# Moving one quarter of a tile's maxima and two query copies ahead of a value copy, and one cast from ScalarE to GpSimd

## The chip, the cores and the metric

The kernel runs on one core of a Trainium2 chip. The core has five engines that run side by side and meet at semaphores: TensorE (PE in the profile; PEld is its weight load), VectorE (DVE), ScalarE (ACT), GpSimd (POOL) and SyncE (SP, which here only issues DMAs). TensorE writes its results to PSUM, which has eight banks of 128 x 512 float32; the other data lies in SBUF. The metric is the time of one execution on the device, in microseconds, as the median of several runs; lower is better.

## The reference

A cross-attention layer with a residual and a layer norm, all in float32: four batches of 2048 query rows and 77 context rows, width 512, 16 heads of 32.

```python
qs = (x @ wq).reshape(B, 2048, 16, 32).transpose(0, 2, 1, 3)
ks = (ctx @ wk).reshape(B, 77, 16, 32).transpose(0, 2, 1, 3)
vs = (ctx @ wv).reshape(B, 77, 16, 32).transpose(0, 2, 1, 3)
scores = einsum('bhqd,bhkd->bhqk', qs, ks) / sqrt(32)
scores = where(mask, -inf, scores)
attn = einsum('bhqk,bhkd->bhqd', softmax(scores), vs)
out = attn.transpose(0, 2, 1, 3).reshape(B, 2048, 512) @ wo + x
return (out - mean(out)) / sqrt(var(out) + 1e-5) * gamma + beta
```

## The kernel before

The 8192 query rows are 64 tiles of 128 rows. Two tiles make a block, four tiles a group: the query projection runs by groups, scores and softmax by tiles, the product with the values by blocks. Large products are made in three passes: each float32 operand is split into a rounded high part (float32r) and the rest, and high x high, high x low and low x high are added up in one PSUM bank. So each piece of the transposed input is first cast (the high part, on ScalarE) and then subtracted (the low part, on GpSimd).

The order of the work is written out by hand. `ORDER` is a long string of words, and the program issues them one after the other; each engine runs its own part of them strictly in that order, and waits at semaphores only where data or a buffer is not ready. A word is a letter and a number, for some with a part behind a dot. Those that matter here:

- `Qn`: TensorE projects one quarter (128 columns) of a query group into a PSUM bank, n = 4 x group + quarter. `qn`: VectorE copies that bank to SBUF (line 305). `q5` and `q7` are the quarters 1 and 3 of group 1, which is tiles 4 to 7.
- `Sn`: TensorE makes the scores of tile n (line 428). Its outer loop runs over the four query quarters, so the second round needs quarter 1. The scores of a tile fill four banks; the inner loop `j` runs over these banks.
- `Tn.p`: VectorE adds the mask to a quarter of tile n's heads and takes the negated row maxima, four heads, each one instruction and a short read of its accumulator (line 445). A part empties one of the tile's four banks. `en.p`: ScalarE's exponentials of that quarter (line 460).
- `rn`, `nn`, `tn`: reciprocal (VectorE, line 470), normalising multiplication (GpSimd, line 475) and 32x32 transposition (VectorE, line 496) of tile n. `Pb.i` is one of twelve small DMAs that regroup a block's transposed weights into the tile `PT` (line 507); the ending `s` says that SyncE issues it.
- `Bn`: TensorE projects the values into a bank (line 353; line 341 for the left-over rows of `B2`). `Dn`: VectorE copies that bank to SBUF (line 360). `Zn`: a DMA puts rows of that copy in their place in `vsb` (line 372).
- `Gn`: VectorE makes the low part of `wo` (line 396). `gn`: SyncE loads half a group of the transposed input. `in`: the cast of that half (`cast_xT`, line 270), n = 2 x group + half. `jn`: GpSimd's subtraction for it (line 274). `i7` is the second half of group 3.
- `On`, `Vb`, `+n` are the output projection, the product with the values and the residual of the main stretch.

PSUM banks and SBUF buffers are handed out in the order of the calls by a fixed table (`SLOTS`); TensorE must wait until the last reader of a bank is done before it writes the bank anew. By that table the scores of tile 4 (`S4`) take as their fourth bank that of `B0`, which `D0` empties. `S6` takes the banks of `Q7`, of a quarter of tile 3's scores (the one that `T3.0` reads), of `Q5` and of `B2`. `B1` takes the first bank of `S4`, which `T4.0` empties.

Of the kernel before, what the change touches and what calls it, by code (L numbers as in the profile page):

```python
# [9 lines left out]
F32R = mybir.dt.float32r  # L10
# [7 lines left out]
P = 128  # L18
# [11 lines left out]
NC_D = D // P  # L30
BLK = 256
GRP = 2 * BLK
# [19 lines left out]
E l0 l2 R1 R0 R3 C2 C0 C1 C3 g5 M4.4 A0 M0.1 M12.4 A1 M1.3 A3 M8.4 K2 A2 H2 J3 p K0 g4 J1 i3 i2 S0 I2 j2 S1 T0.1 e0.1  # L52
T0.2 H0 T0.0 j3 e0.0 T1.0 T0.3 e0.2 T1.1 Q4 T1.2 e0.3 F0 T1.3 I0 e1.2 r0 n0 S2 q4 e1.0 S3 T2.3 T2.0 Q7 i5 T2.1 e1.3 F2
T2.2 j5 t0 e1.1 Q6 i4 F1 g7 r1 Y1 e2.0 F3 L1 T3.2 n1 Q5 x1 T3.1 e2.1 Y0 q6 R2 T3.3 e3.3 j4 t1 B0 e2.3 P0.6s x3 e3.1 B2
D0 i7 q7 Z0.s T3.0 P0.10s e3.0 q5 P0.2s S4 P0.7s D2 e3.2 Z3.s S6 T4.0 P0.4s e2.2 G1 B1 g6 G2 Z1.s G0 Z2.s T4.3 e4.3
P0.3s r3 G3 P0.0s Q9 n3 T4.1 P0.1s T4.2 e4.2 P0.9s D1 P0.8s r2 n2 e4.0 t3 P0.5s Q8 P0.11s e4.1 T6.0 T6.3 i6 t2 Q10
e6.0 r4 P1.0s T6.2 n4 P1.8s T6.1 e6.1 S5 P1.2s q10 x2 q8 Q11 e6.2 j6 P1.11s T5.3 P1.1s T5.2 e5.3 P1.10s T5.1 P1.9s t4
j7 e6.3 P1.4s S7 P1.6s Q14 T7.0 P1.7s e7.0 q9 P1.3s r6 T7.3 P1.5s n6 e7.3 T7.2 x0 q11 Q13 g8 e7.2 T5.0 Z13.s T7.1 g9
# [120 lines left out]
def xattn_layernorm(  # L179
# [15 lines left out]
    nc = tc.nc  # L195
# [12 lines left out]
    def buf(shape, dtype, tag, name):  # L208
        pool = tiny if shape[-1] <= H else sb
        return pool.tile(shape, dtype, tag=tag + next(slots[tag]), name=name)  # L210

    def once(held, key, shape, dtype, tag):
        if key not in held:
            held[key] = buf(shape, dtype, tag, f"{tag}_{key}")
        return held[key]
# [42 lines left out]
    fx, xh, xl, qd, qp, pts, m8s, mbs = {}, {}, {}, {}, {}, {}, {}, {}  # L258
# [6 lines left out]
    def load_xT(g, c):  # L265
        fx[g, c] = buf([P, 2, GRP], F32, "xtf", name=f"xtf_{g}_{c}")
        nc.sync.dma_start(fx[g, c], xT[g, :, c : c + 2])

    def cast_xT(g, c):
        nc.scalar.copy(once(xh, g, [P, NC_D, GRP], F32R, "xth")[:, c : c + 2], fx[g, c])  # L270

    def split_xT(g, c):
        l = once(xl, g, [P, NC_D, GRP], F32R, "xtl")
        nc.gpsimd.tensor_tensor(l[:, c : c + 2], fx.pop((g, c)), xh[g][:, c : c + 2].bitcast(F32), ALU.subtract)  # L274
# [19 lines left out]
    def q_visit(g, m):  # L294
        pq = qp[g, m] = bank(f"pq_{g}_{m}")
        if g:
            q_rows(pq, m, g, slice(0, GRP))
        else:
            for i in range(2):
                q_rows(pq[:, i * BLK : (i + 1) * BLK], m + i, 0, slice(BLK, GRP))  # L300

    def q_evac(g, m):
        pq = qp.pop((g, m))
        if g:
            nc.vector.tensor_copy(once(qd, g, [P, NG, GRP], F32, "q")[:, m, :], pq)  # L305
        else:
            nc.vector.tensor_copy(qd[0][:, m : m + 2, BLK:], pq.rearrange("p (m r) -> p m r", m=2))
# [456 lines left out]
    for c in range(0, NC_D, 2):  # L764
# [11 lines left out]
        "L": lambda k, part: load_mask(k), "M": mask_bias,  # L776
        "l": lambda k, part: nc.sync.dma_start(fx[1, k], xT[1, :, k : k + 2]),
        "g": lambda k, part: load_xT(k // 2, k % 2 * 2),
        "i": lambda k, part: cast_xT(k // 2, k % 2 * 2), "j": lambda k, part: split_xT(k // 2, k % 2 * 2),
        "Q": lambda k, part: q_visit(*divmod(k, 4)), "q": lambda k, part: q_evac(*divmod(k, 4)),  # L780
        "S": lambda k, part: scores(k), "T": lambda k, part: maxima(k, q4 * part, q4 * part + q4),
        "e": lambda k, part: exps(k, q4 * part, q4 * part + q4), "r": lambda k, part: recip(k),
# [73 lines left out]
```

## Time and profile before

| what | value |
|---|---|
| median of 3 runs | 507.34 us (507.14 to 507.61) |
| the profiled execution | 507.4 us, its span 505.6 us |
| mean granted TensorE clock | 0.994 |
| PE busy | 495.3 us, 98% of the span |
| DVE busy | 468.3 us, 93% |
| ACT busy | 474.1 us, 94% |
| POOL busy | 414.2 us, 82% |
| chain that ended last | PE 82%, DVE 12%, POOL 3% |

The span goes from the first to the last instruction that the profile holds; the execution's own time is 1.8 us longer. Busy time of PE counts matmuls whose ends are modelled, so a short wait can be partly covered by the modelled end of the matmul ahead of it. In the timelines each row starts with the start (us from the start of the span) and the duration; a bracket at the end gives the idle time of the engine ahead of the row and what ended it. Rows of one engine overlap a little, since an instruction's write-back is still counted while the next one has begun; the pitch from start to start tells what one costs in a row of several. One matmul of line 428 leaves two records in the trace (64 in all for the scores of a tile).

### The profile page before, as it was taken

The numbers are of one execution on the slowest core, as the hardware profiler recorded it, in microseconds if no ns is written. First come the engines' busy times: TensorE is split into PE (matmuls) and PEld (weight loads), VectorE is DVE, ScalarE is ACT, GpSimd is POOL, SyncE is SP. The second block draws the span as 40 slices with busy tenths as digits, with TensorE's granted clock in tenths as the row PEclk, the third lists the DMA queues.
The fourth block names the chain that finished last, engine by engine and source line by source line (L and its number), as shares of the span: only waits on it lengthen the run. The fifth ranks groups of instructions, "written<-read, shape, count | busy, mean of one in ns | idle before, by whom it ended". The sixth has DMA issues, their size and how long they took to land.

```text
span 505.6 us, 21827 instructions
## 1 busy us (share of the span) xinstructions
PE 495.3 (98%) x6834; PEld 383.1 (76%) x6834; DVE 468.3 (93%) x2556; ACT 474.1 (94%) x2253; POOL 414.2 (82%) x379
## 2 busy tenths in 40 slices
PE   9999999999999999999999999999999999999993
PEld 6987777777777787777777777777877777877672
DVE  6797999999999999999999999999999999999995
ACT  6699999998999999999999999999999999999972
POOL 3663756999978998988899898889989769889894
PEclk9999999999999999999999999999999999999997
DMA  8947767878987777777777777778777788678656
GB/s 312 396 151 213 177 188 179 240 193 234 258 234 216 213 221 200 219 231 232 212 208 221 208 200 234 226 211 241 223 195 234 199 229 236 182 205 203 182 172 252
DMA packets 59521, 110.97 MB, mean 219 GB/s; under 512 B 9441, under 2 KB 12283, under 8 KB 59410
## 3 DMA queue, kind: packets, MB, share of 16 engines
q1 hardware_dynamic: 56658, 103.99, 70.8%
q0 software_dynamic: 2224, 5.05, 3.6%
q8 instruction: 60, 0.98, 0.9%
q10 hardware_dynamic: 528, 0.52, 0.4%
q14 instruction: 51, 0.42, 0.3%
HBM read 41.79 MB, written 16.78 MB: 116 GB/s over the span
## 4 chain that ended last, share of the span: by engine, by line
PE 82%; DVE 12%; POOL 3%; issue 1%; DMA 1%; ACT 1%; DVEq 0%; POOLq 0%
PE pq L291 31%; PE po L602 28%; PE sc L428 9%; PE pa L521 9%; DVE pbuf L445 4%; DVE B L496 3%; PE pk L314 1%; PE pq L745 1%; PE pv L353 1%; DVE q L305 1%; DVE AL L554 1%; POOL pbuf L475 1%; DMA first_xtl<-xw 1%; POOL PT L507 1%; POOL xth L641 1%
## 5 line engine op out<-in xcount | busy, mean ns | idle before, releaser
L460 ACT ACTIVATE pbuf<-pbuf,nm 128x77 f32<-128x77 f32 x1024 | 352.5, 351 | 3.4 <-DVE nm L445 3.3
L460 ACT ACTIVATION_READ_ACCUMULATOR pbuf<-pbuf,nm 128x1 f32 x1024 | 195.7, 191 | 0.0
L445 DVE CUSTOM_DVE_ANT_0 pbuf<-sc,mb 128x77 f32<-128x77 f32 x1024 | 171.1, 233 | 6.9 <-PE sc L428 3.7
L475 POOL TENSOR_TENSOR pbuf<-pbuf,ri 128x1232 f32<-128x1232 f32 x63 | 142.8, 2268 | 32.0 <-DVE ri L470 30.7
L602 PE MATMUL po<-woh,AH 128*128 128x512 f32 x256 | 101.6, 397 | 0.0
L291 PE MATMUL pq<-xth,wqh 128*128 128x512 f32 (+1 forms) x256 | 101.3, 396 | 0.2
L602 PE MATMUL po<-wol,AH 128*128 128x512 f32 x256 | 99.8, 390 | 0.0
L291 PE MATMUL pq<-xth,wql 128*128 128x512 f32 (+1 forms) x256 | 98.1, 383 | 0.0
L291 PE MATMUL pq<-xtl,wqh 128*128 128x512 f32 (+1 forms) x256 | 98.0, 383 | 0.0
L496 DVE STREAM_TRANSPOSE B<-pbuf 128x1280 f32<-128x1280 f32 x64 | 96.2, 1503 | 1.7 <-POOL pbuf L475 0.6
L602 PE MATMUL po<-woh,AL 128*128 128x512 f32 x256 | 93.1, 390 | 0.1
L445 DVE DVE_READ_ACCUMULATOR2_ANT nm<- 128x1 f32 x1024 | 84.7, 83 | 0.0
L274 POOL TENSOR_TENSOR xtl<-xtf,xth 128x1024 fp32r<-128x1024 f32 x28 | 67.2, 2404 | 4.3 <-ACT xth L270 4.3
L641 POOL TENSOR_TENSOR o<-o,bet 128x512 f32<-128x512 f32 x51 | 65.9, 1294 | 3.8
L428 PEld LDWEIGHTS sc<-kct,q 32*64 32x64 f32 x4096 | 51.5, 130 | 22.8 <-issue 11.1
L641 POOL TENSOR_TENSOR o<-o,gam 128x512 f32<-128x512 f32 x51 | 67.1, 1316 | 0.0
L428 PE MATMUL sc<-kct,q 32*64 32x77 f32 x4096 | 61.0, 238 | 0.4 <-DVE q L305 0.4
L521 PE MATMUL pa<-PT,vsb 96*32 96x256 f32 x992 | 59.5, 382 | 0.0
L602 PEld LDWEIGHTS po<-woh,AH 128*128 128x128 f32 x256 | 48.0, 188 | 12.6 <-issue 1.2
L291 PEld LDWEIGHTS pq<-xth,wqh 128*128 128x128 f32 x256 | 48.1, 188 | 12.3 <-issue 1.4
L602 PEld LDWEIGHTS po<-woh,AL 128*128 128x128 f32 x256 | 47.9, 188 | 11.0 <-DVE AL L554 1.1
L291 PEld LDWEIGHTS pq<-xth,wql 128*128 128x128 f32 x256 | 48.1, 188 | 9.8
(134 smaller groups left out, 637.3 us busy)
## 6 DMA issues: line engine op xcount, KB each, us to landing
PT<-B SPq DMA_DIRECT2D x351, 128.0 KB
xtf<-xT SPq DMA_DIRECT2D x28, 512.0 KB
o<-x SPq DMA_DIRECT2D x56, 256.0 KB
out<-o SPq DMA_DIRECT2D x56, 256.0 KB
PT<-B POOLq DMA_DIRECT2D x20, 128.0 KB, 3.9
PT<-B SPq DMA_DIRECT2D x17, 64.0 KB
stage_a<-wk SPq DMA_DIRECT2D x4, 256.0 KB
stage_a<-xT SPq DMA_DIRECT2D x2, 512.0 KB
```

Of the source, the lines that this page charges most:

```text
L274: nc.gpsimd.tensor_tensor(l[:, c : c + 2], fx.pop((g, c)), xh[g][:, c : c + 2].bitcast(F32), ALU.subtract)
L291: nc.tensor.matmul(pq, w[:, c, m * P : (m + 1) * P], r[g][:, c, rs], start=(n == 0), stop=(n == 11))
L305: nc.vector.tensor_copy(once(qd, g, [P, NG, GRP], F32, "q")[:, m, :], pq)
L314: nc.tensor.matmul(pks[m][:, : NB * NK], w[:, c, m * P : (m + 1) * P], ctx_s[c][i], start=(c == 0 and n == 0), stop=(c == NC_D - 1 and n = ...
L428: mm = nc.tensor.matmul(sc[j][r0 : r0 + SR, g * NK : (g + 1) * NK], qs[q, g, rs.start + r0 : rs.start + r0 + SR], kct[q, g, t // TPB, keys ...
L445: nc.vector.tensor_tensor_reduce(pb[:, h // 2, (h % 2) * NK : (h % 2 + 1) * NK], scs[t][j][:, g * NK : (g + 1) * NK], mb[:, t % TPB, keys_ ...
L460: nc.scalar.activation(pb[:, h // 2, (h % 2) * NK : (h % 2 + 1) * NK], pb[:, h // 2, (h % 2) * NK : (h % 2 + 1) * NK], AF.Exp, bias=nmax[t ...
L475: nc.gpsimd.tensor_tensor(pv, pv, rv.to_broadcast((P, NP, 2, NK)), ALU.mult)
L496: nc.vector.transpose(bt.rearrange("p c q r -> p q c r"), pbuf[t % NPB].rearrange("p q (c r) -> p q c r", c=5),)
L521: nc.tensor.matmul(pas[b, g // 2][HD * j : HD * (j + 1), (g % 2) * BLK : (g % 2 + 1) * BLK], vsb[:, 2 * b // TPB, h % 2, HD * (h // 2) : H ...
L602: nc.tensor.matmul(pos[t], a[:, c, rs], w[:, c, :], start=(first and i == 0), stop=(i == len(terms) - 1))
L641: nc.gpsimd.tensor_tensor(od[t], od[t], (gam, bet)[i], (ALU.mult, ALU.add)[i])
```

## The change

It makes two edits, both at work that runs within the first tenth of the span, near 40 us; nothing is added to the computation or taken from it.

The first is in `ORDER`. `T3.0`, `q5` and `q7` now stand ahead of `D0` (before: `D0`, `q7`, `T3.0`, `q5`). The second replaces `i7`, the ScalarE cast, by a new word `[7`, which makes the same cast with GpSimd's `tensor_copy`.

```diff
-D0 i7 q7 Z0.s T3.0 P0.10s e3.0 q5 P0.2s S4 P0.7s D2 e3.2 ...
+T3.0 q5 q7 D0 [7 Z0.s P0.10s e3.0 P0.2s S4 P0.7s D2 e3.2 ...
...
-    def cast_xT(g, c):
-        nc.scalar.copy(once(xh, g, [P, NC_D, GRP], F32R, "xth")[:, c : c + 2], fx[g, c])
+    def cast_xT(g, c, eng=nc.scalar):
+        hi = once(xh, g, [P, NC_D, GRP], F32R, "xth")[:, c : c + 2]
+        (eng.copy if eng is nc.scalar else eng.tensor_copy)(hi, fx[g, c])
...
+        "[": lambda k, part: cast_xT(k // 2, k % 2 * 2, nc.gpsimd),
```

The new kernel has one line more, so a line L445 of before is L446 there.

On VectorE, between the transposition of tile 1 (`t1`) and the first maxima of tile 4 (`T4.0`), there stood before (`v` is the copy of a value bank, `pv` that bank, `q` and `pq` the same for the queries, `sc` a bank of scores; ISA is the maxima instruction, and the row without an input its accumulator read; the three further pairs like it are left out):

```order
L496 STREAM_TRANSPOSE B_661<-pbuf_81 128x8x5x32
L360 COPY v_786<-pv_752 128x512
L305 COPY q_572<-pq_3_623 128x512
L445 ISA pbuf_80,nm_701<-sc_0_578,mb_297 128x77
L445 ISA nm_701 128x1
...
L305 COPY q_572<-pq_1_707 128x512
L360 COPY v_840<-pv_777 128x256
```

and now there stands:

```order
L497 STREAM_TRANSPOSE B_661<-pbuf_81 128x8x5x32
L446 ISA pbuf_80,nm_701<-sc_0_578,mb_297 128x77
L446 ISA nm_701 128x1
...
L306 COPY q_572<-pq_1_707 128x512
L306 COPY q_572<-pq_3_623 128x512
L361 COPY v_792<-pv_752 128x512
L361 COPY v_840<-pv_777 128x256
```

The first value copy moved behind the maxima and both query copies; the last row, `D2`, kept its place.

On GpSimd, around the last subtraction for group 2 (`j4`, the second row), there stood before (`xtl` and `xth` are the low and the high part of the transposed input, `xtf` the input as loaded; the rows with `pbuf` and `ri` are normalisations):

```order
L475 TENSOR_TENSOR pbuf_81<-pbuf_81,ri_690 128x8x154
L274 TENSOR_TENSOR xtl_659<-xtf_0_339,xth_644 128x1024
L475 TENSOR_TENSOR pbuf_80<-pbuf_80,ri_923 128x8x154
L475 TENSOR_TENSOR pbuf_82<-pbuf_82,ri_958 128x8x154
L475 TENSOR_TENSOR pbuf_81<-pbuf_81,ri_1015 128x8x154
```

and now there stands:

```order
L476 TENSOR_TENSOR pbuf_81<-pbuf_81,ri_690 128x8x154
L275 TENSOR_TENSOR xtl_659<-xtf_0_339,xth_644 128x1024
L271 CAST xth_794<-xtf_2_688 128x1024
L476 TENSOR_TENSOR pbuf_80<-pbuf_80,ri_923 128x8x154
L476 TENSOR_TENSOR pbuf_82<-pbuf_82,ri_958 128x8x154
```

The cast stands behind that subtraction and ahead of the normalisation of tile 3 (`pbuf_80`). On ScalarE it stood among the exponentials of tile 3, behind `e3.1` and ahead of `e3.0`, and is gone there. The order of matmuls on TensorE and of DMAs on SyncE is the same in both.

More of the change, by code (lines that the diff above doesn't have):

```diff
@@ L54 @@
 T2.2 j5 t0 e1.1 Q6 i4 F1 g7 r1 Y1 e2.0 F3 L1 T3.2 n1 Q5 x1 T3.1 e2.1 Y0 q6 R2 T3.3 e3.3 j4 t1 B0 e2.3 P0.6s x3 e3.1 B2
-D0 i7 q7 Z0.s T3.0 P0.10s e3.0 q5 P0.2s S4 P0.7s D2 e3.2 Z3.s S6 T4.0 P0.4s e2.2 G1 B1 g6 G2 Z1.s G0 Z2.s T4.3 e4.3
+T3.0 q5 q7 D0 [7 Z0.s P0.10s e3.0 P0.2s S4 P0.7s D2 e3.2 Z3.s S6 T4.0 P0.4s e2.2 G1 B1 g6 G2 Z1.s G0 Z2.s T4.3 e4.3
 P0.3s r3 G3 P0.0s Q9 n3 T4.1 P0.1s T4.2 e4.2 P0.9s D1 P0.8s r2 n2 e4.0 t3 P0.5s Q8 P0.11s e4.1 T6.0 T6.3 i6 t2 Q10
@@ L778, in xattn_layernorm @@
         "g": lambda k, part: load_xT(k // 2, k % 2 * 2),
-        "i": lambda k, part: cast_xT(k // 2, k % 2 * 2), "j": lambda k, part: split_xT(k // 2, k % 2 * 2),
+        "i": lambda k, part: cast_xT(k // 2, k % 2 * 2), "[": lambda k, part: cast_xT(k // 2, k % 2 * 2, nc.gpsimd), "j": lambda k, part: split_xT(k // 2, k % 2 * 2),
         "Q": lambda k, part: q_visit(*divmod(k, 4)), "q": lambda k, part: q_evac(*divmod(k, 4)),
```

## The prediction

> **What bounds the kernel now.** I read the page first, then one stretch of the main part, then TensorE's waits, the chain, and last the timelines around 40 us.
>
> ```profile
> span 505.6 us, 21827 instructions
> PE 495.3 (98%) x6834; PEld 383.1 (76%) x6834; DVE 468.3 (93%) x2556; ACT 474.1 (94%) x2253; POOL 414.2 (82%) x379
> ```
>
> ```profile
> 150.00:200.00 50.00, 50.00 (x652) 39.20 (x651) 47.33 (x273) 49.05 (x240) 45.35 (x38) 1.00 0.73 210
> ```
>
> The columns of the second are the stretch, its length, and the busy time of PE, PEld, DVE, ACT and POOL, then TensorE's granted clock, the share of the DMA engines and GB/s. TensorE is busy for 50.00 of 50.00 us at full clock; ScalarE comes next with 49.05. What lets TensorE through earlier at the start therefore carries to the main part, if the others can follow. That they can is seen in their waits over the whole span:
>
> ```profile
> DVE o L605 <- PE po L602: 9.2, 20, 0.8
> ```
>
> ```profile
> ACT o L634 <- POOL rn L628: 5.7, 17, 0.4
> ```
>
> VectorE waits for TensorE 20 times, 9.2 us in all, and ScalarE loses 5.7 us in 17 waits, about 0.34 us each, spread over the blocks; so both have some slack in each block. TensorE itself has, over the whole span, only four waits that the profile names:
>
> ```profile
> PE pw L703 <- PEq L847: 0.9, 1, 0.9
> PE pa L536 <- DVE po L608: 0.4, 1, 0.4
> PE sc L428 <- DVE q L305: 0.4, 1, 0.4
> PE pq L745 <- DVE xth L737: 0.3, 1, 0.3
> ```
>
> The third is the place of the change: scores wait for a query copy. The chain in order of time passes through it:
>
> ```profile
> 38.42 2.73 PE pv L353 x12
> ...
> 41.17 0.69 DVE v L360
> ...
> 43.09 0.61 DVE q L305
> ...
> 43.75 1.64 PE sc L428 x76
> ...
> 397.37 0.88 PE sc L428 x53
> 398.25 2.94 PE pq L291 x12
> ...
> 401.21 0.69 DVE q L305
> ```
>
> The value product ends, VectorE copies it (`D0`), then come `q7`, the maxima and `q5`, and only then `S4` goes on. From 43.75 to 398 us nearly every piece of the chain is TensorE's; at 401.21 VectorE takes over, released by a projection. So a shift of TensorE at 43.75 should reach 401, and what follows starts from there.
>
> **VectorE's part.** The timeline of VectorE:
>
> ```profile
> 36.42 0.68 DVE L305 COPY q<-pq 128x512 f32<-128x512 f32 x1
> 37.02 0.22 DVE L445 CUSTOM_DVE_ANT_0 pbuf<-sc,mb 128x77 f32<-128x77 f32 x1
> ...
> 37.65 1.50 DVE L496 STREAM_TRANSPOSE B<-pbuf 128x1280 f32<-128x1280 f32 x1
> 41.17 0.69 DVE L360 COPY v<-pv 128x512 f32<-128x512 f32 x1 [2.02 <-PE pv L353]
> 41.78 0.68 DVE L305 COPY q<-pq 128x512 f32<-128x512 f32 x1
> 42.38 0.23 DVE L445 CUSTOM_DVE_ANT_0 pbuf<-sc,mb 128x77 f32<-128x77 f32 x1
> ...
> 43.01 0.69 DVE L305 COPY q<-pq 128x512 f32<-128x512 f32 x1
> 43.61 0.41 DVE L360 COPY v<-pv 128x256 f32<-128x256 f32 x1
> 44.56 0.24 DVE L445 CUSTOM_DVE_ANT_0 pbuf<-sc,mb 128x77 f32<-128x77 f32 x1 [0.53 <-PE sc L428]
> ```
>
> VectorE stands idle for 2.02 us after the transposition, since `D0` is next in its order and waits for the value bank. Behind it are queued three pieces that need nothing new: tile 3's other maxima ran from 37.02 on, so its scores were there, and the projections stand ahead of the value product, which is under way at 38.42. By pitch, `T3.0` costs 43.01 - 42.38 = 0.63, `q5` 43.61 - 43.01 = 0.60 and `q7` 42.38 - 41.78 = 0.60, together 1.83 us, and the idle stretch holds 2.02. From 37.65 + 1.50 = 39.15 they end at 40.98 and `D0` still starts at 41.17, with 0.19 to spare. So the move costs `D0` nothing, and its cover is that idle time; if the pieces took 0.2 more, `D0` would slip by the excess.
>
> **What TensorE gains.**
>
> ```profile
> 41.07 1.95 PE L341 MATMUL pv<-stage_b,ctx_r 128*64 128x256 f32 x16
> 42.95 0.39 PE L428 MATMUL sc<-kct,q 32*64 32x77 f32 x16
> 43.75 1.62 PE L428 MATMUL sc<-kct,q 32*64 32x77 f32 x112 [0.41 <-DVE q L305]
> 45.42 0.47 PE L353 MATMUL pv<-wvh,ctx_h 128*128 128x512 f32 x1
> ```
>
> `S4` begins at 42.95, directly behind `B2`, makes its first round (16 of 64 records, quarter 0 of the queries) and stops for quarter 1, which `q5` delivers at about 43.70. The bracket says 0.41, but it counts from the modelled end of the last matmul. A whole tile's scores take 0.88 (the chain at 397.37), so a round takes 0.22 and the next was due at 42.95 + 0.22 = 43.17: the loss is 43.75 - 43.17 = 0.58 us. It cannot be under 0.41, the idle time, nor above 0.80, the whole distance of the two rows; I take 0.58, since the 0.88 shows the pitch of the same work undisturbed. With the copies done at 40.98 nothing holds the second round. The fourth bank of `S4` needs `D0`, which ends near 41.86: 1.1 us early.
>
> What is late next? `S6` needs the bank of `D2`. `D2` now waits for `B2`'s end (41.07 + 1.95 = 43.02) and runs to about 43.45; `S6` starts at 42.95 + 0.88 = 43.83. `T4.0` waited for `S4` before (0.53) and does so again: 44.56 - 0.58 = 43.98, when VectorE has been free for half a microsecond. `B1` needs the bank that `T4.0` empties; four maxima at 0.63 end the reads near 44.7, and `B1` starts at 45.42 - 0.58 = 44.84, as close behind as before. All that follows on VectorE hangs on `T4.0`, and GpSimd's next normalisation on VectorE's reciprocal, so all of it comes 0.58 earlier. The value 0.58 thus goes whole into the sum.
>
> **The cast.**
>
> ```profile
> 41.49 1.03 ACT L270 CAST xth<-xtf 128x1024 fp32r<-128x1024 f32 x1
> 42.65 0.36 ACT L460 ACTIVATE pbuf<-pbuf,nm 128x77 f32<-128x77 f32 x1
> ...
> 47.34 0.36 ACT L460 ACTIVATE pbuf<-pbuf,nm 128x77 f32<-128x77 f32 x1 [0.47 <-DVE nm L445]
> ```
>
> ```profile
> 31.10 2.88 POOL L274 TENSOR_TENSOR xtl<-xtf,xth 128x1024 fp32r<-128x1024 f32 x1 [0.78 <-ACT xth L270]
> 34.77 2.58 POOL L475 TENSOR_TENSOR pbuf<-pbuf,ri 128x1232 f32<-128x1232 f32 x1 [0.79 <-DVE ri L470]
> 37.31 2.40 POOL L274 TENSOR_TENSOR xtl<-xtf,xth 128x1024 fp32r<-128x1024 f32 x1
> 48.03 4.76 POOL L475 TENSOR_TENSOR pbuf<-pbuf,ri 128x1232 f32<-128x1232 f32 x2 [8.31 <-DVE ri L470]
> ```
>
> ScalarE saves 42.65 - 41.49 = 1.16 us there, since the maxima it needs (`T3.0`) now come at about 39.8. But twelve exponentials later it waits for `T4.3`, before for 0.47, and `T4.3` comes only 0.58 earlier: the wait grows to about 1.05 and the saving is lost in it. Worth to the sum: 0. GpSimd has no cast from float32 to float32r in this trace. Below, the cast cannot cost less than nothing; above, the nearest row is the subtraction of the same shape and output type, which reads two tensors, 2.40 (2.88 beside VectorE). I take 2.4: from 39.71 to 42.1, in the idle stretch of 8.31 us that ends with the reciprocal, now due at 47.45. The cast would have to take over 7.7 us to show. Its reader, the subtraction `j7`, comes after that normalisation in GpSimd's order and is not moved ahead. So 0 again; no DMA is issued by the moved steps.
>
> SyncE's order is unchanged:
>
> ```profile
> 41.90 0.74 SPq L372 DMA_DIRECT2D vsb<-v  x1
> 42.69 1.96 SPq L507 DMA_DIRECT2D PT<-B  x3
> ```
>
> `Z0` at 41.90 waits for `D0` and the regrouping DMAs queue behind it. With `D0` where it was, they stay where they were: no gain, and no loss.
>
> The same GpSimd rows bear on a rule of the Trainium skill, in SBUF — State Buffer, section "Who interferes with whom": GpSimd shares a port pair with VectorE, and a VectorE instruction with two SBUF inputs and a GpSimd instruction that reads SBUF shut each other out for a whole instruction, while one with at most one SBUF input, outside the two-port modes, is not held. By it the three moved pieces, whose source is PSUM, run beside the cast, and the sum stays. The trace agrees as far as it goes: the copy at 36.42 and the four maxima from 37.02 have pitches of 0.60 and 0.63 with GpSimd busy from 34.77 to 39.71.
>
> **Sum.** 507.4 (the profiled execution; 505.6 of span and 1.8 around it) - 0.58 + 0 + 0 = 506.8 us. The profiled execution lies 0.06 above the median of the runs, 507.34, which is inside their spread; the median would become 506.76.
>
> **Rivals.**
>
> *Given back.* TensorE starts `B1` 0.58 earlier but loses it again before 401 us, because something fed by SyncE does not move: `Z0` and the DMAs behind it stay, and the first product with the values needs them. Time: 507.4 - 0.58 + 0.58 = 507.4, as before. For it: SyncE's rows are dense from 41.90 on. Against it: TensorE names no wait there before, and VectorE and ScalarE show slack in each block. Chance 0.14.
>
> *The cast holds VectorE* (the other side). If GpSimd's cast shut VectorE out from 39.71 to 42.1, `T3.0` would just be done, `q5` and `q7` would follow to 43.3, and `D0` would run from 43.3 to 44.0. TensorE stops at the fourth bank of `S4`, still in its first round, until about 44.05 instead of 42.95: 1.10 lost where before 0.58 was, so 507.4 + 0.52 = 507.9. It decides from the point where `D0` ends later than 42.95 + 0.58 = 43.53. Against it speak the pitches of 0.60 and 0.63 beside GpSimd; for it, that no row has a cast there. Chance 0.06.
>
> *ScalarE sets the pace.* At 49.05 of 50 us ScalarE is nearly full, and if it, not TensorE, paced the main part, the whole 1.03 us of the cast would count: 507.4 - 1.03 = 506.4. Against it: its 5.7 us of waits and TensorE's 50.00 of 50.00. Chance 0.07.
>
> **How the numbers follow.** The forecast, 506.8, has a chance of 0.66, and 0.07 is left for what I do not see, in both directions. Its own range is 506.5 to 507.1, from the bounds 0.41 and 0.80 of the stall and the spread of about 0.25 to either side that the runs show. The range 506.2 to 507.6 takes in that, most of "given back" with the same spread, and most of "ScalarE sets the pace"; it leaves out the second rival, the edges and the unforeseen, together just under 0.2. A difference of 0.2% is 1.0 us, about what a measurement of this kernel can tell from no change: the limits are 506.3 and 508.4. Under 506.3 lie half of "ScalarE sets the pace" (0.035), the low edge of the forecast (0.05) and half of the unforeseen (0.035), in all 0.12. Over 508.4 lie the other half of that and the upper edge of "the cast holds VectorE", 0.05. The rest, 0.83, is within.
>
> **What would show it.** Right: `T3.0`, `q5`, `q7` on VectorE between 39.1 and 41.0, `D0` at 41.17 still released by TensorE with an idle time of 0.2 or so; scores of `S4` and `S6` in one row of 128 records from 42.95; `B1` near 44.84; the wait of L428 for a query copy gone from TensorE's list; a cast on GpSimd of about 2.4 us at 39.7; ScalarE's wait ahead of `T4.3`'s exponentials at about 1 us; VectorE's first chain piece near 400.6. Wrong: `D0` later than 41.4, `B1` still near 45.4, a new wait of TensorE between 45 and 401, or a cast on GpSimd that reaches 47 us.

## The result and the profile after

The changed kernel takes 506.85 us in the median of 19 runs (505.96 to 508.16), the kernel before 507.76 us on the same chip (19 runs, 507.14 to 508.81). The ratio is 0.9981, with a 95% interval from 0.9974 to 0.9989: 0.96 us less, between 0.56 and 1.32. The forecast was a gain of 0.58.

The profiled execution took 507.38 us. The page's head, and the shares of the chain that ended last:

```profile
span 505.5 us, 21829 instructions
PE 496.0 (98%) x6834; PEld 383.8 (76%) x6834; DVE 468.4 (93%) x2556; ACT 473.1 (94%) x2252; POOL 414.5 (82%) x380
...
PE 96%; POOL 1%; DMA 1%; ACT 1%; DVE 0%; issue 0%; DVEq 0%
```

ScalarE has one instruction fewer and GpSimd one more. The chain is TensorE's to 96%, where VectorE held 12% before. That share differs from execution to execution and says little about the change: it is 83%, with 12% for VectorE, in a second profile of this kernel (`e4` below), and 96% in a kernel with the order of before (`e6`). TensorE's waits, as total, count and longest:

```profile
PE pw L704 <- PEq L848: 0.9, 1, 0.9
PE pa L537 <- DVE po L609: 0.5, 1, 0.5
PE pq L746 <- DVE xth L738: 0.3, 1, 0.3
```

Scores no longer wait for a query copy. This execution began late: in the chain in order of time, the first key projection (`pk`) starts at 11.51 us, before at 10.99. Over all the executions profiled here that start moved by up to a microsecond, whatever the kernel. So times near 40 us are compared by distances. The timelines of VectorE and TensorE after the change:

```profile
38.17 1.51 DVE L497 STREAM_TRANSPOSE B<-pbuf 128x1280 f32<-128x1280 f32 x1
39.60 0.20 DVE L446 CUSTOM_DVE_ANT_0 pbuf<-sc,mb 128x77 f32<-128x77 f32 x1
...
40.21 1.28 DVE L306 COPY q<-pq 128x512 f32<-128x512 f32 x2
41.69 0.69 DVE L361 COPY v<-pv 128x512 f32<-128x512 f32 x1 [0.21 <-PE pv L354]
43.58 0.42 DVE L361 COPY v<-pv 128x256 f32<-128x256 f32 x1 [1.20 <-PE pv L342]
44.45 0.24 DVE L446 CUSTOM_DVE_ANT_0 pbuf<-sc,mb 128x77 f32<-128x77 f32 x1 [0.44 <-PE sc L429]
```

```profile
43.46 1.84 PE L429 MATMUL sc<-kct,q 32*64 32x77 f32 x128
45.32 0.47 PE L354 MATMUL pv<-wvh,ctx_h 128*128 128x512 f32 x1
```

The maxima and both copies fill the idle stretch, `D0` starts when TensorE releases it, 0.21 us after VectorE was free, and the scores of tiles 4 and 6 run as one row of 128 records. From the first score to `B1` it is 45.32 - 43.46 = 1.86 us; before it was 45.42 - 42.95 = 2.47. The cast on GpSimd and ScalarE's wait:

```profile
40.19 1.04 POOL L271 CAST xth<-xtf 128x1024 fp32r<-128x1024 f32 x1
47.92 4.75 POOL L476 TENSOR_TENSOR pbuf<-pbuf,ri 128x1232 f32<-128x1232 f32 x2 [6.69 <-DVE ri L471]
```

```profile
47.23 0.36 ACT L461 ACTIVATE pbuf<-pbuf,nm 128x77 f32<-128x77 f32 x1 [1.02 <-DVE nm L446]
```

The end of the program shows a difference that the prediction did not look for. Both halves of the last output tile are made by VectorE; ScalarE issues the store of the first half (ACTq), SyncE that of the second (SPq). First the timeline of before, then of after:

```profile
500.46 0.88 DVE L685 SCALAR_TENSOR_TENSOR xtl<-po,mvt,bet 128x256 f32<-128x256 f32 x2
501.31 0.36 ACTq L691 DMA_DIRECT2D out<-xtl  x1
501.71 0.33 SPq L691 DMA_DIRECT2D out<-xtl  x1
```

```profile
500.71 0.88 DVE L686 SCALAR_TENSOR_TENSOR xtl<-po,mvt,bet 128x256 f32<-128x256 f32 x2
501.27 0.36 ACTq L692 DMA_DIRECT2D out<-xtl  x1
501.97 0.33 SPq L692 DMA_DIRECT2D out<-xtl  x1
```

Before, ScalarE issues its store 0.85 us after VectorE began the first half; now after 0.56. SyncE's store comes 0.37 and 0.38 us after VectorE's end, the same in both. From VectorE's end to the end of the span it is 505.6 - 501.34 = 4.3 us before and 505.5 - 501.59 = 3.9 after. The earlier store alone does not explain this: in the profiles of the experiments below, the same stretch is 4.3 (`e1`) or 3.9 (`e3`, `e5`, `e7`) where ScalarE's store is late, and 3.6 to 3.9 where it is early.

### The profile page after: what moved, and what is told of

Read it like the earlier page. It is cut to its first block, busy times and chain, and to the rows that moved or that the text cites. A ratio compares the mean times of both kernels' runs of the same rounds, so it can differ in the third digit from the quotient of the medians.

```text
span 505.5 us, 21829 instructions
## 1 busy us (share of the span) xinstructions
PE 496.0 (98%) x6834; PEld 383.8 (76%) x6834; DVE 468.4 (93%) x2556; ACT 473.1 (94%) x2252; POOL 414.5 (82%) x380
## 4 chain that ended last, share of the span: by engine, by line
PE 96%; POOL 1%; DMA 1%; ACT 1%; DVE 0%; issue 0%; DVEq 0%
PE pq L292 35%; PE po L603 34%; PE pa L522 11%; PE sc L429 11%; PE pq L746 1%; PE pk L315 1%; PE pv L354 1%; DMA first_xtl<-xw 1%; POOL xth L642 1%; PE pv L342 0%; POOL mvt L666 0%; ACT AH L551 0%; PE pa L537 0%; DVE xtl L682 0%; ACT xth L674 0%
## 5 line engine op out<-in xcount | busy, mean ns | idle before, releaser
L446 DVE CUSTOM_DVE_ANT_0 pbuf<-sc,mb 128x77 f32<-128x77 f32 x1024 | 171.2, 234 | 6.9 <-PE sc L429 3.7
L446 DVE DVE_READ_ACCUMULATOR2_ANT nm<- 128x1 f32 x1024 | 85.6, 84 | 0.0
```

The lines of the kernel that those rows point to most:

```text
L446: nc.vector.tensor_tensor_reduce(pb[:, h // 2, (h % 2) * NK : (h % 2 + 1) * NK], scs[t][j][:, g * NK : (g + 1) * NK], mb[:, t % TPB, keys_ ...
```

## The experiments

Each kernel ran beside runs of the kernel before on the same chip. Times are given as the difference to it in us, from the ratio and its interval.

### The order alone, the cast alone, one copy alone, and the change again

`e1_order_only` leaves the cast on ScalarE:

```diff
-T3.0 q5 q7 D0 [7 Z0.s P0.10s e3.0 ...
+T3.0 q5 q7 D0 i7 Z0.s P0.10s e3.0 ...
```

> Only the order on VectorE is changed (T3.0, q5, q7 ahead of D0); the cast stays on ScalarE. The measure in the trace is the distance from the first scores of S4 to the first matmul of B1: 2.47 us before, 1.86 us with the whole change. Theory A, the stall of S4 is all there is: 1.86 again, and the same time as the whole change, about 0.6 us under before. Theory B, the relief of ScalarE brings the part of the measured 0.9 us beyond that: 1.86 too, but the time some 0.3 us above the whole change. ScalarE's wait ahead of tile 4's last quarter is near zero to 0.1 us under either (1.02 less the 1.03 of the cast).

Measured: 0.51 us less (0.00 to 1.07), ratio 0.9990 [0.9979, 1.0000]. On TensorE:

```profile
43.38 1.84 PE L428 MATMUL sc<-kct,q 32*64 32x77 f32 x128
45.23 0.47 PE L353 MATMUL pv<-wvh,ctx_h 128*128 128x512 f32 x1
```

The distance is 1.85, as in the whole change: the stall is the order's doing alone. ScalarE shows no wait ahead of `T4.3`'s exponentials, as expected. The interval of the time takes in what either theory gave, so the time does not choose between them.

`e2_cast_only` keeps the old order and moves the cast:

```diff
-D0 i7 q7 Z0.s T3.0 ...
+D0 [7 q7 Z0.s T3.0 ...
```

> Only the cast moves to GpSimd; VectorE keeps D0, q7, T3.0, q5. Theory A: the distance from S4 to B1 stays at 2.47 us, and the time is that of before within the noise (0.0 us). Theory B: the distance stays, but the time falls by about 0.3 us. In the trace ScalarE runs out of work before T3.0's exponentials, since T3.0 comes as late as before.

Measured: 0.20 us less (-0.20 to 0.66), ratio 0.9996 [0.9987, 1.0004]. TensorE's waits keep their row, and the end of the program is that of the whole change:

```profile
PE sc L429 <- DVE q L306: 0.4, 1, 0.4
```

```profile
500.72 0.88 DVE L686 SCALAR_TENSOR_TENSOR xtl<-po,mvt,bet 128x256 f32<-128x256 f32 x2
501.28 0.36 ACTq L692 DMA_DIRECT2D out<-xtl  x1
```

The store goes out 0.56 us after VectorE's start, with the cast alone; in `e1`, with the order alone, it is 0.85. So the earlier store belongs to the cast, not to the order.

`e3_swap_only` only puts `q5` ahead of the maxima; `D0` stays first:

```diff
-D0 i7 q7 Z0.s T3.0 P0.10s e3.0 q5 P0.2s S4 ...
+D0 i7 q7 q5 Z0.s T3.0 P0.10s e3.0 P0.2s S4 ...
```

> The smallest edit that brings q5 in time: before, with q5 ahead of T3.0 and all else as it was (D0, q7, q5, T3.0; cast on ScalarE). VectorE's idle 2.0 us ahead of D0 stays. Theory A: q5 ends near 43.0 where S4's second round is due at 43.17 (times as in the trace of before), so the distance from S4 to B1 falls to about 1.9 us and the time by 0.5 to 0.6 us, as with the whole change. If instead the idle time ahead of D0 is what counts, the distance stays near 2.4 and the time at that of before.

Measured: 0.30 us less (-0.20 to 0.81), ratio 0.9994 [0.9984, 1.0004].

```profile
42.98 2.04 PE L428 MATMUL sc<-kct,q 32*64 32x77 f32 x128
44.94 0.50 PE L353 MATMUL pv<-wvh,ctx_h 128*128 128x512 f32 x1
```

The distance is 1.96, most of the way to 1.86: what counted was `q5` being ready in time, and `D0` was not in the way of that. The time, whose interval takes in zero, would not tell this by itself.

`e4_after_again` is the changed kernel once more, beside these three.

> The changed kernel again, beside the others on the same chip. Theory A: 0.6 us under before, a ratio of 0.9988; theory B: 0.9 us under, 0.9982. Distance from S4 to B1 1.86 us. The trace also tells whether the 0.52 us by which its first stage ran late in the first profile is of the kernel or of that one execution: of the execution, the first projection ends as in the trace of before.

Measured: 1.22 us less (0.76 to 1.62), ratio 0.9976 [0.9968, 0.9985], in agreement with the 0.96 of the first time. The distance is 45.07 - 43.23 = 1.84. TensorE's first key projection starts 0.27 us later than in the profile of before, not at the same time as expected and not 0.52 later as in the first profile; so that lateness goes with the execution.

### Is it ScalarE's time, or only the place of its last instructions?

If the 1.03 us that ScalarE is freed of counted, an instruction that takes no time should not matter. `e5_after_nop` adds an empty ScalarE instruction to the change, where the cast stood; `e6_before_nop` adds one to the kernel before, behind `i7`:

```diff
 e5: "[": lambda k, part: (cast_xT(k // 2, k % 2 * 2, nc.gpsimd),
+                          nc.scalar.nop(hint="pad")),
 e6: "i": lambda k, part: (cast_xT(k // 2, k % 2 * 2),
+                          nc.scalar.nop(hint="pad") if k == 7 else None),
```

> The changed kernel with one empty instruction on ScalarE where the cast used to stand, so that ScalarE's program is as long as before. In the traces so far ScalarE issues the last store 0.36 us after VectorE has finished its data where the cast is on ScalarE, and 0.08 us after where it is not; the missing 0.29 us then stands between this store and the instruction behind it. Theory C, the place of the store in ScalarE's instruction stream decides: 0.36 again, and a time about 0.3 us above the changed kernel (as with the order alone, ratio 0.999). Theory B, the freed ScalarE time brings the rest: 0.08 stays, and the time is the changed kernel's (0.998).

> Before, with one empty instruction on ScalarE behind the cast; ScalarE does no less work than before. Theory C: the pause of 0.29 us moves one instruction forward, in front of a wait that lasts 2.5 us and hides it, so the last store is issued 0.08 us after its data as in the changed kernel, and the time is about 0.3 us under before (0.9994); the distance from S4 to B1 stays at 2.47. Theory B: 0.36 stays, and the time is that of before.

Measured: `e5` 0.46 us less than before (-0.10 to 1.01), ratio 0.9991 [0.9980, 1.0002]; `e6` 0.36 less (-0.10 to 0.81), ratio 0.9993 [0.9984, 1.0002]. The end of the program, first in `e5`, then in `e6`:

```profile
500.03 0.88 DVE L686 SCALAR_TENSOR_TENSOR xtl<-po,mvt,bet 128x256 f32<-128x256 f32 x2
500.88 0.36 ACTq L692 DMA_DIRECT2D out<-xtl  x1
```

```profile
500.31 0.88 DVE L685 SCALAR_TENSOR_TENSOR xtl<-po,mvt,bet 128x256 f32<-128x256 f32 x2
500.87 0.36 ACTq L691 DMA_DIRECT2D out<-xtl  x1
```

With the empty instruction the change has the old 0.85 again, although ScalarE is still freed of the cast; the kernel before gets the new 0.56 by the empty instruction, although ScalarE has the cast. The distance from tile 4's first score to `B1` stays 1.85 in `e5` and 2.47 in `e6`. So it is not ScalarE's work: a pause of 0.29 us sits at one place of its instruction stream, and one instruction more or fewer decides whether the last store stands ahead of it or behind it. The times alone could not show this 0.3: each of the intervals of `e2`, `e5` and `e6` takes in zero.

The same was tried on SyncE: `e8_after_sp_nop` adds an empty SyncE instruction to the change, and `e12_after_sp_nop_2` is the same kernel run again.

```diff
 "[": lambda k, part: (cast_xT(k // 2, k % 2 * 2, nc.gpsimd),
+                      nc.sync.nop(hint="pad")),
```

> The changed kernel with one empty instruction on SyncE near 42 us, where SyncE waits anyway. SyncE's last store also comes 0.37 us after its data in all traces so far. Theory C, applied to SyncE: with the pause one instruction earlier, in front of a wait of 1.3 us, the store comes 0.08 us after its data, and the time falls by 0.1 to 0.3 us under the changed kernel. If the 0.37 is something else, it stays, and the time with it.

> The change with one empty instruction added on SyncE, run again with more rounds. Theory (one instruction more on SyncE moves the pause of about 0.3 us that stood ahead of SyncE's last store behind it; ScalarE's last store already goes out early in the change): SyncE's last store is issued about 0.3 us sooner after VectorE's last result than in the change, and lands sooner by as much; the time is up to 0.3 us under the change's, about 1.2 us under before. Rival (the landing of the other store sets the end, or the two collide when issued closer together): the time is the change's, about 0.96 us under before.

Measured: `e8` 0.51 us less than before (-0.25 to 1.27), ratio 0.9990 [0.9975, 1.0005]; `e12` 0.36 less (-0.10 to 0.81), ratio 0.9993 [0.9984, 1.0002]. The end of `e12`:

```profile
499.88 0.88 DVE L686 SCALAR_TENSOR_TENSOR xtl<-po,mvt,bet 128x256 f32<-128x256 f32 x2
500.44 0.36 ACTq L692 DMA_DIRECT2D out<-xtl  x1
500.84 0.33 SPq L692 DMA_DIRECT2D out<-xtl  x1
```

SyncE's store now follows VectorE's end (500.76) after 0.08 us instead of 0.38, so the pause exists there too and moves in the same way. But the gain of 1.2 us that the theory gave lies outside the interval. The store is issued earlier and the time is not shown to be shorter; why, the runs don't settle, and this is no better version.

The traces show more of the pause than these ends do. Count all of SyncE's records in order of their start, from 0, with the semaphore waits that the timeline leaves out: in each of the fourteen traces a gap of 0.34 to 0.46 us lies ahead of records 79, 207, 335, 463, 591 and 719, which stand 128 apart, while every other such series of records 128 apart has a gap under 0.06 in it. The last store of SyncE is record 719 in the change and 720 in `e8` and `e12`, where record 719 is the semaphore wait ahead of it. So the pause comes by the count of instructions, whatever they are. What makes it is not shown.

### Does a shift of TensorE at 45 us reach the end?

`e7_b1_twice` is the kernel before with the twelve matmuls of `B1` made twice, a known delay at the same place:

```diff
+        for again in range(2 if g == 1 else 1):
+            n = 0
             for c in range(NC_D):
                 for i, v in ((0, wvh), (0, wvl), (1, wvh)):
```

> Before, with the twelve matmuls of B1 made twice into the same bank (same result), so that TensorE is 12 x 0.227 = 2.72 us later from 48 us on. It measures how much of a shift of TensorE at this place reaches the end. If TensorE paces all that follows: 2.7 us more time, 510.3. If other engines or DMAs pace a part: less. The shift of every later visit of TensorE against before tells where it would be lost.

Measured, from four runs: 3.65 us more (2.69 to 4.62), ratio 1.0072 [1.0053, 1.0091]. Matmul by matmul against before, the delay is 2.67 us at 48 us and between 2.43 and 2.71 on to 489 us. So it carries. At the very end a wait is added that before does not have:

```profile
494.31 1.08 PE L539 MATMUL pa<-PT,vsb 96*32 96x128 f32 x32 [1.53 <-DMA PT<-B]
```

A regrouping DMA of the last block comes late for TensorE. Why it does in this kernel stays open.

### What if D0 does come late?

`e9_d0_late` puts `D0` behind `D2`, so that the bank for tile 4's scores can't be free in time:

```diff
-T3.0 q5 q7 D0 [7 Z0.s P0.10s e3.0 P0.2s S4 P0.7s D2 e3.2 ...
+T3.0 q5 q7 [7 e3.0 S4 D2 D0 Z0.s P0.10s P0.2s P0.7s e3.2 ...
```

> The change with the first value copy D0 put behind the second, D2, so that tile 4's scores surely wait for it. Theory (what the new order is worth is what TensorE no longer loses between tile 4's first score and B1, and a loss there reaches the end whole): the first round of scores reaches its fourth bank after 0.17 us and stops until D0 is done, which can start only behind the left-over product of the values (D2 waits for it) and ends about 1.1 us later than tile 4's first score; the distance from that score to B1, 2.48 us before and 1.85 in the change, becomes about 3.0, and the time stands about 1.1 us above the change and 0.2 above before (the earlier last store taken off). Rival (VectorE's order at this place only decides where TensorE waits, and later slack takes it back): the time is that of the change within 0.3 us.

Measured: 1.57 us more than before (0.71 to 2.49), ratio 1.0031 [1.0014, 1.0049]. TensorE:

```profile
42.78 0.36 PE L429 MATMUL sc<-kct,q 32*64 32x77 f32 x6
43.98 1.67 PE L429 MATMUL sc<-kct,q 32*64 32x77 f32 x122 [0.84 <-DVE v L361]
45.73 0.47 PE L354 MATMUL pv<-wvh,ctx_h 128*128 128x512 f32 x1
...
72.09 0.47 PE L292 MATMUL pq<-xth,wqh 128*128 128x512 f32 x1 [0.33 <-DVE nm L446]
```

The distance to `B1` is 2.95, as expected (3.0); the price was expected at 0.2 above before and came out larger. A second wait, for maxima at 72 us, stands in neither the change nor the kernel before. Counted from TensorE's first key projection, `B1` starts 1.0 us later than the mean of the seven kernels without the stall (see the table below), and the output projection near 182 us 1.6 later: lost time was not taken back but added to. Five of the ten runs lay between 507.3 and 508.6 us and five between 509.7 and 511.0; the profile is one of the first five, so what the others lose on top stays open.

### How much cover does the cast have?

The prediction gave the cast 7.7 us of cover. `e10_cast_x6` and `e11_cast_x10` make it six and ten times:

```diff
+        for again in range(1 if eng is nc.scalar else 6):   # e11: 10
             (eng.copy if eng is nc.scalar else eng.tensor_copy)(hi, fx[g, c])
```

> The change with the GpSimd cast made six times. Theory (the cast lies in GpSimd's idle stretch, of which 6.69 us were left behind one cast of 1.04): five more casts take 5.2 us, the idle time shrinks to about 1.5 us, the normalisation still starts when the reciprocal comes, 47.9 us in the change's profile, and the time is the change's within 0.3 us. Rival (a GpSimd instruction that reads SBUF holds VectorE at a shared port): VectorE's copies and maxima between 40 and 46 us get slower by up to the casts' time, TensorE's distance from tile 4's first score to B1 grows above 1.85 us, and the time by 0.5 us or more.

> The change with the GpSimd cast made ten times. Theory: ten casts of 1.04 us run from 40.2 to 50.6 us, past the reciprocal at 47.9, so the cover of 7.7 us is used up and the normalisations of tiles 3 and 2 come 2.7 us late. GpSimd is busy in some 90% of the main part and can catch up slowly, so some part of it should reach TensorE through the regrouped weights: 0.5 to 2.5 us above the change. Rival (the weights of these tiles are needed so much later that nothing waits for them): the time is the change's within 0.3 us, and no new wait stands in TensorE's list.

Measured: `e10` 0.05 us more than before (-0.51 to 0.56), ratio 1.0001 [0.9990, 1.0011], so 1.0 above the change's 0.96; `e11` (four runs) 2.69 more (2.03 to 3.40), ratio 1.0053 [1.0040, 1.0067], 3.65 above the change. Counted from the first key projection, the output projection near 182 us is 1.2 later in `e10` and 3.6 in `e11` than the mean of those seven kernels, which agrees. `e10` on GpSimd (a cast ahead of, and one beside, VectorE's subtractions), on VectorE and on TensorE:

```profile
44.30 1.04 POOL L272 CAST xth<-xtf 128x1024 fp32r<-128x1024 f32 x1
...
45.40 1.38 POOL L272 CAST xth<-xtf 128x1024 fp32r<-128x1024 f32 x1
```

```profile
43.26 0.42 DVE L362 COPY v<-pv 128x256 f32<-128x256 f32 x1 [1.20 <-PE pv L343]
44.13 0.24 DVE L447 CUSTOM_DVE_ANT_0 pbuf<-sc,mb 128x77 f32<-128x77 f32 x1 [0.45 <-PE sc L430]
...
44.77 1.11 DVE L398 TENSOR_TENSOR wol<-stage_b,woh 128x512 fp32r<-128x512 f32 x1
...
45.80 1.52 DVE L398 TENSOR_TENSOR wol<-stage_b,woh 128x512 fp32r<-128x512 f32 x1
```

```profile
48.70 0.47 PE L293 MATMUL pq<-xth,wqh 128*128 128x512 f32 x1 [0.72 <-DVE nm L447]
```

The copy and the maxima, which read PSUM, take beside the casts what they take without. But `G1`, `G2` and `G0`, three subtractions of `wo` that read two tensors in SBUF, take 3.15 us together; in the change they stand as

```profile
45.09 1.89 DVE L397 TENSOR_TENSOR wol<-stage_b,woh 128x512 fp32r<-128x512 f32 x3
```

The first starts at 44.77 and ends at 45.88, 0.54 behind the end of the cast (45.34): it seems to wait out the cast and then take its usual 0.6. The cast at 45.40 is itself drawn out to 46.78, and the next subtraction ends 0.54 behind it. Behind the subtractions stand the maxima `T4.3` that empty the bank for `Q9`, and TensorE waits 0.72 us there. The distance from tile 4's first score to `B1` did not grow (1.86). In `e11` the casts reach past VectorE's fourth subtraction and past the reciprocal:

```profile
39.65 12.34 POOL L272 CAST xth<-xtf 128x1024 fp32r<-128x1024 f32 x10
```

```profile
49.31 0.47 PE L293 MATMUL pq<-xth,wqh 128*128 128x512 f32 x1 [1.54 <-DVE nm L447]
...
59.34 0.87 PE L430 MATMUL sc<-kct,q 32*64 32x77 f32 x56 [1.30 <-DVE nm L447]
```

Two waits of TensorE, 1.54 and 1.30, make up 2.84 of the 3.65. Both name VectorE's maxima, but only the first goes back to the subtractions, which take 3.96 us there. Ahead of the second, VectorE's transposition waits for a late normalisation, and VectorE works without a break from it to the maxima that TensorE waits for:

```profile
54.24 1.51 DVE L498 STREAM_TRANSPOSE B<-pbuf 128x1280 f32<-128x1280 f32 x1 [2.24 <-POOL pbuf L477]
```

So the theory's late normalisations do reach TensorE, with 1.30 us inside its 0.5 to 2.5, though through VectorE's order and not through the regrouped weights. In `e10` the theory's "no change" fell, and the rival had the price right but the wrong instructions: not copies and maxima, but the subtractions with two inputs in SBUF.

This is the case that the Trainium skill describes in SBUF — State Buffer, "Who interferes with whom": such an instruction and a GpSimd one that reads SBUF exclude each other for a whole instruction, while one with at most one SBUF input, outside the two-port modes, is not held. These traces agree on both halves, 0.42 for the copy and 1.52 instead of 0.63 for the subtraction.

## Why the prediction was right, and where it was not

**The stall, 0.58.** Right. By distances it is 2.47 - 1.86 = 0.61, and the order alone gives it (`e1`). `D0` stayed where TensorE releases it, with 0.21 to spare (0.19 forecast).

**That it carries.** Mostly right. The table has, for several profiled executions, the time from the first matmul of the first key projection to four later ones: `B1`, an output projection near 182 us, a query projection near 407 us and a value product near 489 us, from the timelines of TensorE.

| kernel | B1 | near 182 | near 407 | near 489 |
|---|---|---|---|---|
| before | 34.59 | 171.69 | 396.70 | 478.44 |
| e6 (before, empty instruction) | 34.59 | 171.65 | 396.70 | 478.39 |
| e2 (cast alone) | 34.61 | 171.55 | 396.59 | 478.29 |
| e3 (one copy alone) | 34.17 | 171.07 | 396.51 | 478.20 |
| e5 (after, empty instruction) | 34.35 | 171.33 | 396.41 | 478.14 |
| e1 (order alone) | 33.99 | 170.91 | 395.84 | 477.51 |
| after | 33.97 | 171.09 | 396.46 | 478.19 |
| e4 (after again) | 33.98 | 171.03 | 396.16 | 477.86 |
| e8 (after, SyncE) | 33.95 | 170.85 | 396.03 | 477.76 |
| e12 (after, SyncE) | 34.10 | 171.22 | 396.54 | 478.22 |

At 182 us the seven in which the stall is gone lead the other three by 0.56 on average (171.07 against 171.63), at 489 us by 0.39 (477.98 against 478.37), while single executions of the same order differ by up to 0.7 there. So "given back" fell for the larger part: of the 0.56, 0.39 is left at 489 us, some two thirds, which is a rough figure with that scatter. `e7`'s known delay of 2.67 kept at least 2.43.

**The hand-over at 401 us** did not show in the first profile of the change. The chain at that place reads

```profile
398.42 5.68 PE pq L292 x24
404.10 0.88 PE sc L429 x54
```

and is TensorE's on to 490 us. But the second profile of the same kernel, `e4`, has it:

```profile
397.95 2.96 PE pq L292 x12
400.94 0.69 DVE q L306
```

Counted from the first key projection that is 389.84, before 401.21 - 10.83 = 390.38: 0.54 earlier, near the 0.58 forecast. The chain of `e6`, with the order of before, has no hand-over there either. So whether the chain passes through VectorE differs between executions of one order, probably because the two engines are nearly level there; one chain says little about which engine sets the pace.

**The cast on GpSimd, 2.4 us.** Mis-sized: it took 1.04. The nearest row, a subtraction, reads two tensors. The sum was not touched, since both sizes are covered. **Its cover, 7.7 us,** was the step that failed: it counted only GpSimd's own next work. That limit is real, as the second wait of `e11` shows, but another comes first: by `e10` the cover ends where VectorE's subtractions begin, at 45.09, 4.9 us behind the cast's start at 40.19. The 4.9 is read from these rows; no run with two to five casts tests it.

**ScalarE's part, 0.** The saving went into the wait ahead of `T4.3`, 1.02 us (1.05 forecast), as said. But "worth 0" left out the end of the program: one instruction fewer on ScalarE let the last store go 0.29 us earlier. That is shown by the rows of `e2`, `e5` and `e6`. Its worth in time is only bounded: the two kernels with the earlier store alone gained 0.20 and 0.36, the two with the order and the late store 0.51 and 0.46, the change itself 0.96 and 1.22. The means of the parts, 0.28 and 0.48, add up to 0.76, inside the interval of the change; but `e8` and `e12`, which have both, gained only 0.51 and 0.36, and the stretch at the end of the span scatters by as much as the store moved. So how the 0.96 splits stays open.

**The rivals.** "The cast holds VectorE" did not happen, since the pieces beside one cast read PSUM, but its mechanism is real and begins 4.9 us later. "ScalarE sets the pace" fell: `e2` takes the whole cast from ScalarE and gains 0.20, at most 0.66, and not 1.03.

The time of 506.85 came out next to 506.8 partly by chance: the median of the kernel before was higher over its 19 runs (507.76) than over the first three of them, which the forecast went by (507.34), and the gain was larger.

## What to carry to other kernels

When an in-order engine stands idle for a known release, pull into that stretch what another engine will wait for, and check by pitch that it fits: here 1.83 us of work in 2.02 us of idle time took the whole stall away. Ask also for the smallest move that does it: one copy put ahead of the maxima (`e3`), with the idle stretch left as it was, already shortened the distance by 0.51 of the 0.61. When work moves to an idle engine, its cover ends at that engine's next work or at the first instruction of a neighbour that it excludes, whichever is earlier. Compare the last rows of the span too: taking an instruction away far ahead can shift when a store at the end goes out.

## What the runs showed of the hardware

A pause of 0.29 us moves past ScalarE's last store when a single instruction is taken out or put in some 460 us earlier, even an empty one (0.85 against 0.56 us from VectorE's start to the store); SyncE's last store shows the same (0.38 against 0.08). In SyncE's records such a gap, 0.34 to 0.46 us, comes every 128 records in all fourteen traces. GpSimd's cast of 128x1024 from float32 to float32r takes 1.04 us, as ScalarE's (1.03), against 2.40 for its subtraction of that shape. Beside VectorE's subtractions the same cast takes 1.38, and a subtraction up to 1.52 instead of 0.63.
